# A graph-network layer on one Trainium2 core: twelve consecutive edge tiles per half of a chunk, and loads grouped to match

## Chip, cores and metric

The kernel runs on one core of a Trainium2 chip. The metric is the device time of one execution in microseconds (us); the median of several runs counts.

## The reference

There are N = 12,500 nodes with 160 features (64 scalars, 32 vectors of three) and E = 400,000 edges, sorted by destination. Cut to what matters:

```python
h_s, h_v = s @ lin1_ws * a / sqrt(64), einsum(v, lin1_wv) * a / sqrt(32)   # per node
w  = silu(edge_scalars @ fc_w1 / 8) @ fc_w2 / 8                            # per edge, 224 weights
es, ev = h_s[edge_src], h_v[edge_src]                                      # gather, random rows
mid_s, mid_v = products of w, es, ev with edge_attr (e0, e1)               # messages
agg = segment_sum(mid, edge_dst) / 4                                       # to the destinations
pre = sc(s, v) + lin2(agg) * a
out = layernorm(x + concat(silu(pre_s[:, :64]), sigmoid(pre_s[:, 64:]) * pre_v))
```

## The kernel before

Edges are cut into 3125 tiles of 128. Three consecutive tiles make a block (`BT = 3`, 1042 blocks, each 384 edges by destination), and a block's destinations are taken to lie within a window of 16 nodes from its first one. A chunk has 24 tiles in two halves of twelve (`SIDE`), since the edge scalars have 64 rows and two halves fill 128 partitions (`es`). A step (`steps`) takes a quad: two neighbouring slots of each half. `tile_of` says which tile sits in a slot: in before, half 0 holds the even blocks and half 1 the odd ones, in groups of three tiles. The last five tiles are put into steps of their own. There are 782 steps.

**Start.** Node tables are computed block by block (`h_tab`, 12,500 rows of 640 bytes, written to DRAM by ACT's queue). Meanwhile POOL gathers the source rows of 25 quads from `x` itself (`raw_rows`, L360, 100 gathers; their columns of `src` come with `load_raw_columns`, L241 to L250); these quads are turned into rows of `h` later, in the steps 30, 60, ... 750 (`raw_stages`). `rel`, the destination within the window, is computed for all tiles at once (`relative`, L510, through `by_slots`).

**Main loop** (from L1232). The order of all engines is written out by hand; each engine works through its queue in that order, and waits come from the data. Per step:
- POOL gathers one row of `h_tab` per edge, one instruction per tile of 128 rows (`gather`, L549), into `hg`, a buffer with four copies (`deep`, `bufs=4`).
- PE multiplies the hidden layer by the weights (`weights`, L561, four matmuls into `pw`); the hidden layer (`hidden`, L540/L542) is made four steps ahead, every second step, from `es`.
- DVE makes the products `pr` (L571, L579), the one-hot of `rel` (`one_hot`, L616) and from it and the edge attributes the selection `sel` (`select_quad`, L630).
- PE sums a tile's messages into its block's window (`sum_up`, `add_tile`, L637). A pair of blocks shares an accumulator `pa`: block b of half 0 in its upper rows, b + 1 of half 1 in its lower ones. When both are complete, ACT copies it out (`close`, L1116), two steps later PE turns it (`turn_blocks`, L646), and after 16 blocks `output` (L662) applies `lin2`; DVE adds each block's result to its window of `acc` (L670).
- Every four tiles of 128 nodes whose blocks are all added (`settled`) are finished in a job of its own (`begin`, `finish`).

21 quads are fetched without POOL: their rows come one by one in small transfers issued by SP and ACT (`Off`, `hs_sp`, `hs_act`, L946), spread over the steps before; `Off.begin` (L901 to L914) loads the four columns of `src` for such a quad, one load per run of consecutive tiles. With the 25 raw quads, 46 steps therefore have no gather on POOL.

SP's queue also carries the edge scalars (`load_chunk`, L217, eight steps ahead, `es` has two copies) and, for `AHEAD` = 60 tiles at a time, the indices `idx` and the edge attributes `eat` (`ahead`, L178/L179, twelve steps ahead; `idx` has two copies, `eat` one). ACT copies `eat` into the order of the slots (`by_slot`, `eas`, L604) when the first tile of a group is needed. The queue of SP is in order: a load that waits for its buffer holds up all loads behind it.

In `load_chunk` a half is four runs of three tiles, each 1.5 KB per row:

```python
            queue.dma_start(
                to[:, :n * P].rearrange("c (q e) -> c q e", e=EB),
                bass.AP(tensor=full.tensor, offset=full.offset,
                        ap=[full.ap[0], [2 * EB, k], [1, EB]]))
```

Of the kernel before, what the change touches and what calls it, by code (L numbers as in the profile page):

```python
# [11 lines left out]
I32 = mybir.dt.int32  # L12
# [4 lines left out]
OP = mybir.AluOpType  # L17
# [4 lines left out]
P = 128  # L22
# [7 lines left out]
BT = 3  # L30
EB = BT * P
W = 16
Q = 4
SB = 4 * BT
SIDE = SB
AHEAD = 5 * SB
NF = 4

MARGIN = 128
# [6 lines left out]
ROW = 4 * D  # L46
# [8 lines left out]
RAW_FIRST = 30  # L55
RAW_EVERY = 30
RAW_STEPS = [RAW_FIRST + RAW_EVERY * r for r in range(RAWS)]
RAW_TILES = (0, 1, 3, 4)
RAW_TILE0 = Q * RAW_FIRST

CYC = [(i, (i + 1) % 3, (i + 2) % 3) for i in range(3)]
# [8 lines left out]
def gnn_kernel(  # L70
# [69 lines left out]
    CT = 2 * SIDE  # L140
    chunks = [(c, (SIDE, SIDE)) for c in range(0, TT - CT + 1, CT)]
    left = len(chunks) * CT
    if left < TT:
        assert BT <= TT - left < 2 * BT
        chunks.append((left, (BT, TT - left - BT)))

    def tile_of(c, half, u):
        return chunks[c][0] + u // BT * 2 * BT + half * BT + u % BT

    steps = []  # L150
    for c, (_, halves) in enumerate(chunks):
# [33 lines left out]
    def index(t):  # L185
        a0, idx, _ = ahead(t)
        return idx[:, t - a0:t - a0 + 1]

    def by_slots(out, of, n, f):


        m = n // SB
        for u in range(2 * BT if m else 0):
            o, i = out[:, u // 2 * Q + u % 2:u // 2 * Q + u % 2 + 1], of[:, u // BT * 2 * BT + u % BT:][:, :1]
            f(bass.AP(tensor=o.tensor, offset=o.offset,
                      ap=[o.ap[0], [SB * o.ap[1][0], m], [2 * o.ap[1][0], 2], *o.ap[2:]]),
              bass.AP(tensor=i.tensor, offset=i.offset,
                      ap=[i.ap[0], [SB * i.ap[1][0], m], [BT * i.ap[1][0], 2], *i.ap[2:]]),
              u // BT * 2, m)
        return m * SB  # L200

    ess = {}

    def load_chunk(c, queue=nc.sync):
        if c in ess:
            return
        t0, halves = chunks[c]
        es = ess[c] = loads.tile([2 * S, SIDE * P], F32, name="es")
        for half, n in enumerate(halves):
            to = es[half * S:(half + 1) * S]  # L210
            e0 = (t0 + half * BT) * P
            if n < BT:
                queue.dma_start(to[:, :n * P], es_t[:, e0:e0 + n * P])
                continue
            k = n // BT
            full = es_t[:, e0:e0 + EB]
# [4 lines that stand above are left out]
# [1 line left out]

    ident = consts.tile([P, P], F32, name="ident")
    make_identity(nc, ident)
    iota_i = consts.tile([P, P], I32, name="iota_i")
    nc.gpsimd.iota(iota_i, pattern=[[1, P]], base=0, channel_multiplier=0)

    eps = consts.tile([P, 1], F32, name="eps")
# [1 line left out]

    assert all(T % 6 == 0 for T in RAW_STEPS)
    raw_of = {T: r for r, T in enumerate(RAW_STEPS)}
    raw_cols = consts.tile([P, RAWS, 5], I32, name="raw_cols")
    hi_of = consts.tile([P, RAWS * Q], F32, name="hi_of")
    lo_rows = consts.tile([RAWS * Q, P], F32, name="lo_rows")
    row_of = consts.tile([P, 1], F32, name="row_of")
# [1 line left out]
    l1v = consts.tile([V3, V3], F32, name="l1v")  # L238
    nc.vector.memset(l1v, 0.0)

    def load_raw_columns(a, b):  # L241

        for r in range(a, b):
            t = steps[RAW_STEPS[r]][2][0][0]
            assert [u for u, _, _ in steps[RAW_STEPS[r]][2]] == [t + k for k in RAW_TILES]
            assert divmod(t, GT) == (r, RAW_TILE0 - 5 * r) and t + 5 <= (r + 1) * GT
        of = src[a][:, RAW_TILE0 - 5 * a:][:, :5]
        nc.sync.dma_start(raw_cols[:, a:b],
                          bass.AP(tensor=of.tensor, offset=of.offset,
                                  ap=[of.ap[0], [P * GT - 5, b - a], [1, 5]]))  # L250

    w1 = consts.tile([2 * S, 2 * S], F32, name="w1")
    nc.vector.memset(w1, 0.0)
# [30 lines left out]
    with tc.tile_pool(name="nodes", bufs=3) as nodes, tc.tile_pool(  # L284
# [45 lines left out]
            nc.vector.tensor_reduce(early, share, AX.X, OP.min)  # L330
            nc.vector.tensor_scalar(early, early, -float(MARGIN), None, op0=OP.is_lt)

        load_raw_columns(0, 4)
        at = consts.tile([P, NT], F32, name="at")
        nc.scalar.dma_start(at, attr)
        l1 = consts.tile([P, P], F32, name="l1")
# [89 lines left out]
        def scale():  # L426

            nc.vector.tensor_copy(iota_p, iota_i)
            part = ends_pool.tile([P, RAWS * Q], I32, name="part")
            parts = part.rearrange("p (r a b) -> p r a b", a=2, b=2)  # L430
            of = bass.AP(tensor=raw_cols.tensor, offset=raw_cols.offset,
                         ap=[raw_cols.ap[0], [5, RAWS], [3, 2], [1, 2]])
            nc.vector.tensor_scalar(parts, of, P.bit_length() - 1, None,
                                    op0=OP.logical_shift_right)
            nc.vector.tensor_copy(hi_of, part)
            nc.vector.tensor_scalar(parts, of, P - 1, None, op0=OP.bitwise_and)
            nc.vector.tensor_copy(lo_of, part)
            diagonal = ends_pool.tile([P, P], F32, name="diagonal")
            nc.vector.tensor_mul(diagonal, ident, iota_p)
            nc.vector.tensor_reduce(row_of, diagonal, AX.X, OP.add)  # L440
            at_c = 0
            for a, b in ((64, 128), (0, 64), (192, 224), (160, 192), (128, 160)):
                nc.vector.tensor_scalar_mul(w2[:, at_c:at_c + b - a], raw[:, a:b],
                                            1.0 / math.sqrt(64))
                at_c += b - a
            for m, of, by in scales:
                nc.vector.tensor_scalar_mul(m, of, by)
# [60 lines left out]
    def relative(out, of, b0, m):  # L508
        l = lo[:, b0:b0 + 1]
        nc.vector.tensor_tensor(  # L510
            out, of, bass.AP(tensor=l.tensor, offset=l.offset,
                             ap=[l.ap[0], [4 * l.ap[1][0], m], [l.ap[1][0], 2]]), op=OP.subtract)

    for t in range(by_slots(rel, dt, TT, relative), TT):
        nc.vector.tensor_tensor(rel[:, slot_of[t]:slot_of[t] + 1], dt[:, t:t + 1],
                                lo[:, t // BT:t // BT + 1], op=OP.subtract)
    ends.close()
# [80 lines left out]
    def by_slot(t):  # L598

        a0, _, eat = ahead(t)  # L600
        if a0 not in sorted_eat:
            n = min(AHEAD, TT - a0)
            eas = loads.tile([P, AHEAD, 4], F32, name="eas")
            m = by_slots(eas, eat, n, lambda o, i, b0, m: nc.scalar.copy(o, i))  # L604
            for k in range(m, n):
                o = slot_of[a0 + k] - a0
                nc.scalar.copy(eas[:, o], eat[:, k])
            sorted_eat[a0] = eas
        return sorted_eat[a0]
# [231 lines left out]
    with tc.tile_pool(  # L841
# [46 lines left out]
        class Off:  # L888
# [11 lines left out]

            def begin(self, T, slots):  # L901

                cols = loads.tile([P, Q], I32, name="cols")
                tiles = [steps[T][2][k][0] for k in slots]
                nc.vector.memset(cols, 0.0) if len(tiles) < Q else None
                k = 0
                while k < len(tiles):
                    g, u = divmod(tiles[k], GT)
                    m = 1
                    while k + m < len(tiles) and tiles[k + m] == tiles[k] + m and u + m < GT:  # L910
                        m += 1
                    nc.sync.dma_start(cols[:, k:k + m], src[g][:, u:u + m])
                    k += m
                return cols  # L914

            def byte(self, cols):

                at_byte = loads.tile([P, Q], F32, name="at_byte", bufs=1)
                nc.vector.tensor_scalar(at_byte, cols, float(ROW), None, op0=OP.mult)
                return at_byte  # L920

            def turn(self, at_byte):
# [196 lines left out]
        def turn_blocks(n, j, sa, beside=nc.scalar.copy):  # L1119
            if not turns:  # L1120
                tts[0] = late.tile([P, 7, NO, W], F32, name="tt", bufs=1)
                tts[1] = late.tile([V, NO, W], F32, name="t3", bufs=1)
            turned(misc_ps, sa, tts[0], tts[1], len(turns), 2, beside)
            turns.extend((2 * j, 2 * j + 1))
            if len(turns) == NO or NB - 2 * j - 2 in (10, 4, 0):
                done = list(turns)
                turns.clear()
                maps_due.append((n + 1, done))
# [28 lines left out]
        def sum_up(n, tiles, pr, sel):  # L1157

            for slot, (t, half, _) in sorted(enumerate(tiles), key=lambda k: (k[1][2], k[1][1])):
                b = t // BT  # L1160
                j = b // 2
                assert b % 2 == half
                if j not in pas:
                    pas[j] = pa_ps.tile([P, 512], F32, name="pa")
                added[b] += 1
                stop = added[b] == min(BT, TT - b * BT)
                add_tile(pas[j], half, sel, slot, pr[:, slot], start=(added[b] == 1), stop=stop)
                if stop:
                    ended.add(b)
                    if {2 * j, 2 * j + 1} <= ended:  # L1170
                        close(j, n)

        def add_up(n):
# [276 lines left out]
```

## Time and profile before

| | |
|---|---|
| median of 3 runs | 3861.9 us (3860.59 to 3872.28) |
| the profiled execution | 3860.29 us, span 3858.5 us |
| busy: PE / DVE / ACT / POOL | 3365.6 / 2450.9 / 1023.9 / 2877.1 us |
| mean granted TensorE clock | 0.951 |
| moved | 430.39 MB, mean 112 GB/s |

The time of an execution is a little longer than its span, which runs from the first to the last instruction. Busy time is what an engine spends inside instructions; the time in which it takes up the next one, or waits, is outside. In the rows of groups the columns are: line, engine, operation, written and read tile with shapes, count, busy time in us and mean in ns, idle time just before and what ended it. In the lists of waits: who waited, what it waited for, us in total, how many times, the longest. In a timeline: start and duration in us, engine, line, operation, and in brackets the idle time before it and what ended it. A `q` behind an engine's name is its queue, which issues transfers.

### The profile page before, as it was taken

The numbers are of one execution on the slowest core, as the hardware profiler recorded it, in microseconds if no ns is written. First come the engines' busy times: TensorE is split into PE (matmuls) and PEld (weight loads), VectorE is DVE, ScalarE is ACT, GpSimd is POOL, SyncE is SP. The second block draws the span as 40 slices with busy tenths as digits, with TensorE's granted clock in tenths as the row PEclk, the third lists the DMA queues.
The fourth block names the chain that finished last, engine by engine and source line by source line (L and its number), as shares of the span: only waits on it lengthen the run. The fifth ranks groups of instructions, "written<-read, shape, count | busy, mean of one in ns | idle before, by whom it ended". The sixth has DMA issues, their size and how long they took to land. (4 is left out here: it accounts for less than half of the span.)

```text
span 3858.5 us, 79139 instructions
## 1 busy us (share of the span) xinstructions
PE 3365.6 (87%) x18417; PEld 1697.8 (44%) x18417; DVE 2450.9 (64%) x6839; ACT 1023.9 (27%) x3246; POOL 2877.1 (75%) x3046
## 2 busy tenths in 40 slices
PE   3588988998988998998898898998999998988897
PEld 3234444444444444444444444444444444444444
DVE  2465666666656666666666566666666666666666
ACT  0222222223222222232222222222222322222222
POOL 7777776777777777777777777777777777777775
PEclk7799999999999999999999999999999999999999
DMA  9744444445445454444544444445454544445442
GB/s 217 222 101 107 106 105 109 103 105 113 105 99 117 102 113 105 110 105 107 112 103 114 104 102 110 105 102 114 103 111 105 113 100 110 112 102 113 107 97 71
DMA packets 328137, 430.39 MB, mean 112 GB/s; under 512 B 96368, under 2 KB 270988, under 8 KB 326764
## 3 DMA queue, kind: packets, MB, share of 16 engines
q0 software_dynamic: 145824, 249.07, 28.7%
q1 hardware_dynamic: 153988, 154.65, 18.1%
q10 hardware_dynamic: 27848, 21.56, 1.9%
q8 instruction: 148, 2.42, 0.3%
q14 instruction: 329, 2.70, 0.2%
HBM read 400.80 MB, written 24.19 MB: 110 GB/s over the span
## 5 line engine op out<-in xcount | busy, mean ns | idle before, releaser
L549 POOL DMA_INDIRECT hg<-h_tab,idx x2938 | 2779.7, 946 | 918.8 <-issue 794.1
L637 PE MATMUL pa<-pr,sel 128*64 128x416 f32 x6250 | 1324.2, 546 | 3.9 <-DVE sel L630 3.9
L579 DVE TENSOR_TENSOR pr<-pw,hg 128x384 f32<-128x384 f32 x2205 | 1090.8, 547 | 0.0
L561 PE MATMUL pw<-w,hid 64*128 64x224 f32 x6250 | 829.9, 384 | 199.5 <-DVE sel L630 170.6
L571 DVE TENSOR_TENSOR pr<-pw,hg 128x512 f32<-128x512 f32 x735 | 507.9, 691 | 723.1 <-DMA hg<-h_tab,idx 688.6
L561 PEld LDWEIGHTS pw<-w,hid 64*128 64x128 f32 x6250 | 548.2, 191 | 471.5 <-DVE sel L630 220.6
L637 PEld LDWEIGHTS pa<-pr,sel 128*64 128x64 f32 x6250 | 392.4, 140 | 578.9 <-issue 537.9
L540 PE MATMUL ph<-es,w 128*128 128x512 f32 (+1 forms) x784 | 457.3, 666 | 36.2 <-DVE acc L1093 29.0
L1116 ACT COPY sa<-pa 128x416 f32<-128x416 f32 x521 | 262.0, 503 | 648.3 <-PE pa L637 591.4
L542 ACT ACTIVATE hid<-ph 128x512 f32<-128x512 f32 x392 | 233.3, 595 | 694.3 <-PE ph L540 389.1
L616 DVE TENSOR_TENSOR pw<-rel,pw 128x64 f32<-128x64 int16 x782 | 175.1, 224 | 347.8 <-PE pw L561 338.8
L646 PE MATMUL pt<-ident,sa 128*128 128x128 f32 (+1 forms) x2084 | 329.7, 281 | 62.0 <-ACT hid L542 36.4
L646 PEld LDWEIGHTS pt<-ident,sa 128*128 128x128 f32 (+1 forms) x2084 | 218.5, 131 | 344.3 <-issue 200.7
L650 ACT COPY tt<-pt 128x192 f32<-128x192 f32 x521 | 165.6, 318 | 643.9 <-PE pt L646 269.8
L662 PE MATMUL po<-tt,l 128*96 128x256 f32 (+3 forms) x1340 | 317.1, 384 | 10.3 <-DVE y L749 4.6
L630 DVE TENSOR_TENSOR sel<-pw,eas 128x256 f32<-128x256 f32 (+1 forms) x757 | 311.8, 412 | 0.2
L662 PEld LDWEIGHTS po<-tt,l 128*96 128x96 f32 x1340 | 211.3, 166 | 121.3 <-issue 48.3
L540 PEld LDWEIGHTS ph<-es,w 128*128 128x128 f32 (+1 forms) x784 | 121.6, 195 | 309.3 <-issue 177.3
L670 DVE TENSOR_TENSOR acc<-acc,os 96x32 f32 x1042 | 194.1, 186 | 21.1 <-ACT os L665 2.6
L360 POOL DMA_INDIRECT raw_rows<-in_x_dram,raw_cols x100 | 95.5, 955 | 35.7 <-issue 27.4
L665 ACT COPY os<-po 96x512 f32<-96x512 f32 (+2 forms) x67 | 38.1, 569 | 274.4 <-PE po L662 271.8
L700 PE MATMUL pp<-ident,acc 96*128 96x96 f32 x190 | 37.4, 282 | 83.4 <-DVE pw L616 65.5
(141 smaller groups left out, 1401.2 us busy)
## 6 DMA issues: line engine op xcount, KB each, us to landing
es<-in_es_t_dram SPq DMA_DIRECT2D x260, 384.0 KB
hs_sp<-h_tab SPq DMA_DIRECT2D x5632, 0.6 KB
hs_act<-h_tab ACTq DMA_DIRECT2D x5376, 0.6 KB
hg<-h_tab,idx POOLq DMA_INDIRECT x2938
raw_tab<-raw_rows ACTq DMA_DIRECT2D x25, 320.0 KB
rg<-raw_tab SPq DMA_DIRECT2D x25, 320.0 KB
h_tab<-ht ACTq DMA_DIRECT2D x6, 1280.0 KB
xt<-in_x_dram SPq DMA_DIRECT2D x23, 320.0 KB
```

The costliest lines, as they stand in the source:

```text
L540: nc.tensor.matmul(ph[:k, c], w1[:k, :k], es[:k, t0 * P + c0 * P:t0 * P + c1 * P], start=True, stop=True)
L542: nc.scalar.activation(hid[:k, c], ph[:k, c], AF.Silu, scale=1.0 / math.sqrt(64))
L549: nc.gpsimd.indirect_dma_start(out=hg[:, t, :], out_offset=None, in_=h_tab, in_offset=bass.IndirectOffsetOnAxis(ap=i, axis=0))
L561: nc.tensor.matmul(pw[:, t, :NWT], hid[r, c * P:(c + 1) * P], w2[r], start=True, stop=True)
L571: nc.vector.tensor_mul(two, pw[:, :n, :2 * S].rearrange("p t (k c) -> p t k c", k=2), hg[:, :n, None, :S].to_broadcast([P, n, 2, S]))
L579: nc.vector.tensor_mul(pr[:, :n, first:first + V3].rearrange("p t (i c) -> p t i c", i=3), pw[:, :n, None, 2 * S + k * V:2 * S + (k + 1) * ...
L630: nc.vector.tensor_mul(sel[:, :n], oh[:, :, None, :].to_broadcast([P, n, 4, W]), e[:, :, :, None].to_broadcast([P, n, 4, W]))
L637: nc.tensor.matmul(pa[half * ROWS:(half + 1) * ROWS, :NPR], sel[:, t].rearrange("p k w -> p (k w)"), pr, start=start, stop=stop)
L646: nc.tensor.transpose(pt[:c, four * P:four * P + k], sa[:k, four * P:four * P + c], ident[:k, :k])
L662: nc.tensor.matmul(po[:, k, :nb], l2[:b, terms[to, part, four]], a[:, :nb], start=(n == 0), stop=(n == len(of) - 1))
L670: nc.vector.tensor_add(window, window, os[:, :, b])
L1116: nc.scalar.copy(sa, pas.pop(j)[:, :NPR])
```

## The change

- **Order of tiles.** In 129 of the 130 chunks each half holds twelve consecutive tiles: blocks 0 to 3 of the chunk's eight in half 0, 4 to 7 in half 1 (`WIDE`, `tile_of`). Blocks b and b + 4 share an accumulator (`place_of`, `pair_blocks`); before it was b and b + 1. The last full chunk and the five tiles behind it keep the old order.
- **Edge scalars.** A half of such a chunk is one run of 6 KB per row.
- **Groups.** `AHEAD` is 72 tiles, three chunks; ACT copies a group's attributes with four strided copies (`by_wide_slots`) where it took six.
- **Columns of a quad.** The four tiles of a quad are now t, t+1, t+12, t+13 (`RAW_TILES`). `Off.begin` loads the 14 columns from t to t+13 in one transfer where they lie in one row group of `src`; `load_raw_columns` does the same for the raw quads, the first two of them in two loads.
- **Relative destinations.** Six strided operations for the wide chunks, and six for the 24 tiles of the last full chunk.
- **Memory.** `iota_i` and `raw_cols` (now 14 columns per quad) move from the constants to the scratch that is freed after the start; `cols` has 14 columns.

```diff
-AHEAD = 5 * SB
+AHEAD = 6 * SB
-RAW_TILES = (0, 1, 3, 4)
+RAW_TILES = (0, 1, SIDE, SIDE + 1)
...
+    WIDE = left // AHEAD * AHEAD // CT
     def tile_of(c, half, u):
+        if c < WIDE:
+            return chunks[c][0] + half * SIDE + u
         return chunks[c][0] + u // BT * 2 * BT + half * BT + u % BT
+    PER = SIDE // BT
+    def place_of(b):
+        if b < 2 * PER * WIDE:
+            return b // (2 * PER) * PER + b % PER, b // PER % 2
+        return b // 2, b % 2
...
+    def by_wide_slots(out, of, n, f):
+        m = n // CT
+        for half in range(2):
+            for k in range(2):
+                f(strided(out, 2 * half + k, [(CT, m), (Q, SIDE // 2)]),
+                  strided(of, half * SIDE + k, [(CT, m), (2, SIDE // 2)]))
...
     def load_chunk(c, queue=nc.sync):
...
+            if c < WIDE:
+                e0 = (t0 + half * SIDE) * P
+                queue.dma_start(to, es_t[:, e0:e0 + SIDE * P])
+                continue
...
-    iota_i = consts.tile([P, P], I32, name="iota_i")
+    iota_i = ends_pool.tile([P, P], I32, name="iota_i")
-    raw_cols = consts.tile([P, RAWS, 5], I32, name="raw_cols")
+    NC = SIDE + 2
+    raw_cols = ends_pool.tile([P, RAWS, NC], I32, name="raw_cols")
...
-        load_raw_columns(0, 4)
+        load_raw_columns(0, 2, 0, 2)
+        load_raw_columns(0, 2, SIDE, 2)
+        load_raw_columns(2, 4)
...
-    for t in range(by_slots(rel, dt, TT, relative), TT):
+    T0 = WIDE * CT
+    for a in range(2):
+        for u in range(BT):
+            u += a * BT
+            nc.vector.tensor_tensor(
+                strided(rel, u // 2 * Q + u % 2, [(CT, WIDE), (2, 2), (BT * Q, SIDE // (2 * BT))]),
+                strided(dt, u, [(CT, WIDE), (SIDE, 2), (2 * BT, SIDE // (2 * BT))]),
+                strided(lo, a, [(2 * PER, WIDE), (PER, 2), (2, SIDE // (2 * BT))]), op=OP.subtract)
+    for t in range(T0 + by_slots(rel[:, T0:], dt[:, T0:], TT - T0,
+                                 lambda o, i, b0, m: relative(o, i, T0 // BT + b0, m)), TT):
...
-            m = by_slots(eas, eat, n, lambda o, i, b0, m: nc.scalar.copy(o, i))
+            if a0 + n <= WIDE * CT:
+                by_wide_slots(eas, eat, n, nc.scalar.copy)
+                m = n
...
             def begin(self, T, slots):
-                cols = loads.tile([P, Q], I32, name="cols")
                 tiles = [steps[T][2][k][0] for k in slots]
+                g, u = divmod(tiles[0], GT)
+                if tiles == [tiles[0] + k for k in RAW_TILES] and u + NC <= GT:
+                    cols = loads.tile([P, NC], I32, name="cols")
+                    nc.sync.dma_start(cols, src[g][:, u:u + NC])
+                    return strided(cols, 0, [(SIDE, 2), (1, 2)])
...
-            turns.extend((2 * j, 2 * j + 1))
+            turns.extend(pair_blocks[j])
...
-                j = b // 2
-                assert b % 2 == half
+                j, of_half = place_of(b)
+                assert of_half == half
-                    if {2 * j, 2 * j + 1} <= ended:
+                    if set(pair_blocks[j]) <= ended:
                         close(j, n)
```

More of the change, by code (lines that the diff above doesn't have):

```diff
@@ L147, in tile_of @@
     def tile_of(c, half, u):
+        if c < WIDE:
+            return chunks[c][0] + half * SIDE + u
         return chunks[c][0] + u // BT * 2 * BT + half * BT + u % BT
+    PER = SIDE // BT
[3 more added lines that the diff above has]
+        return b // 2, b % 2
+    pair_blocks = {}
+    for b in range(NB):
+        j, half = place_of(b)
+        assert half == len(pair_blocks.setdefault(j, []))
+        pair_blocks[j].append(b)
     steps = []
@@ L187, in index, with strided @@
         return idx[:, t - a0:t - a0 + 1]
+    def strided(a, k, dims):
+        a = a[:, k:k + 1]
+        return bass.AP(tensor=a.tensor, offset=a.offset,
+                       ap=[a.ap[0], *[[a.ap[1][0] * d, n] for d, n in dims], *a.ap[2:]])
     def by_slots(out, of, n, f):
@@ L193, in by_slots @@
         for u in range(2 * BT if m else 0):
[L194 to L198, printed above, removed]
+            f(strided(out, u // 2 * Q + u % 2, [(SB, m), (2, 2)]),
+              strided(of, u // BT * 2 * BT + u % BT, [(SB, m), (BT, 2)]),
               u // BT * 2, m)
         return m * SB
+    def by_wide_slots(out, of, n, f):
+        m = n // CT
+        assert m * CT == n
+        for half in range(2):
+            for k in range(2):
+                f(strided(out, 2 * half + k, [(CT, m), (Q, SIDE // 2)]),
+                  strided(of, half * SIDE + k, [(CT, m), (2, SIDE // 2)]))
     ess = {}
@@ L239, in gnn_kernel, with load_raw_columns @@
     nc.vector.memset(l1v, 0.0)
-    def load_raw_columns(a, b):
+    def load_raw_columns(a, b, k=0, n=NC):
         for r in range(a, b):
@@ L245, in load_raw_columns @@
             assert [u for u, _, _ in steps[RAW_STEPS[r]][2]] == [t + k for k in RAW_TILES]
-            assert divmod(t, GT) == (r, RAW_TILE0 - 5 * r) and t + 5 <= (r + 1) * GT
-        of = src[a][:, RAW_TILE0 - 5 * a:][:, :5]
-        nc.sync.dma_start(raw_cols[:, a:b],
+        g, u = divmod(RAW_TILE0 + a * Q * RAW_EVERY + k, GT)
+        assert u - (GT - Q * RAW_EVERY) * (b - a - 1) >= 0 and u + n <= GT
+        of = src[g][:, u:u + n]
+        nc.sync.dma_start(raw_cols[:, a:b, k:k + n],
                           bass.AP(tensor=of.tensor, offset=of.offset,
-                                  ap=[of.ap[0], [P * GT - 5, b - a], [1, 5]]))
+                                  ap=[of.ap[0], [P * GT - (GT - Q * RAW_EVERY), b - a], [1, n]]))
     w1 = consts.tile([2 * S, 2 * S], F32, name="w1")
@@ L431, in scale @@
             of = bass.AP(tensor=raw_cols.tensor, offset=raw_cols.offset,
-                         ap=[raw_cols.ap[0], [5, RAWS], [3, 2], [1, 2]])
+                         ap=[raw_cols.ap[0], [NC, RAWS], [SIDE, 2], [1, 2]])
             nc.vector.tensor_scalar(parts, of, P.bit_length() - 1, None,
@@ L603, in by_slot @@
             eas = loads.tile([P, AHEAD, 4], F32, name="eas")
-            m = by_slots(eas, eat, n, lambda o, i, b0, m: nc.scalar.copy(o, i))
+            if a0 + n <= WIDE * CT:
+                by_wide_slots(eas, eat, n, nc.scalar.copy)
+                m = n
+            else:
+                assert a0 >= WIDE * CT
+                m = by_slots(eas, eat, n, lambda o, i, b0, m: nc.scalar.copy(o, i))
             for k in range(m, n):
@@ L901, in begin @@
             def begin(self, T, slots):
-                cols = loads.tile([P, Q], I32, name="cols")
                 tiles = [steps[T][2][k][0] for k in slots]
+                g, u = divmod(tiles[0], GT)
[3 more added lines that the diff above has]
+                    return strided(cols, 0, [(SIDE, 2), (1, 2)])
+                cols = loads.tile([P, NC], I32, name="cols")[:, :Q]
                 nc.vector.memset(cols, 0.0) if len(tiles) < Q else None
@@ L913, in begin @@
                     k += m
-                return cols
+                return cols.rearrange("p (a b) -> p a b", b=2)
             def byte(self, cols):
                 at_byte = loads.tile([P, Q], F32, name="at_byte", bufs=1)
-                nc.vector.tensor_scalar(at_byte, cols, float(ROW), None, op0=OP.mult)
+                nc.vector.tensor_scalar(at_byte.rearrange("p (a b) -> p a b", b=2), cols,
+                                        float(ROW), None, op0=OP.mult)
                 return at_byte
```

## The prediction

> **What bounds the kernel now.** I read the page first, then the waits and the timeline of POOL, and last the timelines of the start and of the places where POOL stood.
>
> ```profile
> span 3858.5 us, 79139 instructions
> PE 3365.6 (87%) x18417; PEld 1697.8 (44%) x18417; DVE 2450.9 (64%) x6839; ACT 1023.9 (27%) x3246; POOL 2877.1 (75%) x3046
> ...
> L549 POOL DMA_INDIRECT hg<-h_tab,idx x2938 | 2779.7, 946 | 918.8 <-issue 794.1
> L360 POOL DMA_INDIRECT raw_rows<-in_x_dram,raw_cols x100 | 95.5, 955 | 35.7 <-issue 27.4
> ```
>
> PE has the largest busy share, but POOL's 75% misleads: its idle time is nearly all "issue", and 2779.7 busy plus 918.8 idle on L549 make 3698.5 of the 3858.5 us. The timeline and the waits of POOL show what this idle time is (start, duration, engine, and in brackets the idle time before it):
>
> ```profile
> 3.32 1.10 POOL L360 DMA_INDIRECT raw_rows<-in_x_dram,raw_cols  x1 [0.87 <-DMA raw_cols<-in_src_dram]
> ...
> 133.98 0.95 POOL L549 DMA_INDIRECT hg<-h_tab,idx  x1 [0.30 <-issue]
> 135.23 1.89 POOL L549 DMA_INDIRECT hg<-h_tab,idx  x1 [0.30 <-issue]
> ...
> 399.61 0.95 POOL L549 DMA_INDIRECT hg<-h_tab,idx  x1 [0.30 <-issue]
> 400.86 0.95 POOL L549 DMA_INDIRECT hg<-h_tab,idx  x1 [0.30 <-issue]
> ...
> 3831.19 0.94 POOL L549 DMA_INDIRECT hg<-h_tab,idx  x1 [0.30 <-issue]
> ```
>
> ```profile
> POOL hg L549 <- issue: 794.1, 2603, 0.6
> POOL hg L549 <- DMA hg<-h_tab,idx: 43.0, 141, 0.3
> POOL hg L549 <- DVE pr L579: 38.3, 52, 5.1
> ...
> POOL raw_rows L360 <- DMA raw_rows<-in_x_dram,raw_cols: 7.4, 9, 1.6
> ```
>
> POOL issues one gather of 128 rows every 1.25 us (399.61 to 400.86): 0.95 of work and a gap of 794.1/2603 = 0.305. The chain is: first gather at 3.3; 100 x (0.955 + 0.305) = 126.0; 2938 x (0.946 + 0.305) = 3675.4; waits beyond the normal gap, for a free gather buffer 38.3 - 52 x 0.305 = 22.4 and for earlier raw gathers 7.4 - 9 x 0.305 = 4.7. These make 3831.8, and the last gather ends at 3832.1. Behind it lie 26.4 us of last sums and stores. So 98.5% of the span is a count of gathers times a fixed period. Even the step from raw rows to h_tab at 133.98 shows no wait. The other engines matter only where they fall four gather buffers behind: 22.4 us in all.
>
> This execution took 3860.3 us (span 3858.5, 1.8 around it); the median of the runs shown is 3861.9, 1.6 higher. I predict for the median.
>
> **The change part by part.** It removes no gather: the steps, their four tiles and the quads that are fetched otherwise stay as many, so the 3801 us of gathers stay. PE, too, has the same matmuls in the same shapes: two slots per half and step, a pair of blocks closing after the same slots, sixteen blocks per output. Followed through the code's queues, all outputs come at the same steps; of the 24 finishing jobs 15 start one step later, since a pair now holds b and b+4, and the last starts at the same step (773). What is left are loads, small copies and set-up.
>
> ```profile
> q0 software_dynamic: 145824, 249.07, 28.7%
> q1 hardware_dynamic: 153988, 154.65, 18.1%
> ```
>
> ```profile
> L912 SPq DMA_DIRECT2D cols<-in_src_dram x50: 356/422/632, 129.0 to 3633.6; - x50
> ```
>
> *Edge loads.* In 129 chunks each half becomes 64 runs of 6 KB, where it was 256 of 1.5 KB: 258 x 192 = 49,536 runs fewer, the same bytes and issues. The transfer engines are 28.7 + 18.1% busy, so faster loads free no path. The rates per engine, 249.07 MB / (0.287 x 3858.5 x 16) = 14.1 GB/s for the gathers and 13.8 for q1, with its longer and its shorter runs, also leave little to gain. Value 0; the bounds are in the rivals. *SP issues:* by the code 50 column loads become 25, and 75 pairs of idx and eat loads become 68; at the 0.42 us of the row, (25 + 14) x 0.42 = 16 us of SP issue over the whole run, against no POOL wait on idx or cols in its list. Value 0. The shared eat buffer is now reloaded 6 steps after its copies, not 3, so less is queued behind that wait on SP.
>
> ```profile
> L604 ACT COPY eas<-eat 128x40 f32<-128x40 f32 x312 | 44.5, 220 | 19.0 <-issue 17.7 <-DMA es<-in_es_t_dram 1.2
> ```
>
> *Edge attributes.* 312 copies of 40 elements become 43 x 4 = 172 of 72, and 6 short ones for the last group. If one takes as long as before it is 172 x 0.220 = 38 us, if it grows with its elements 172 x 0.396 = 68, against 44.5 now; either is at most 24 us spread over the run, on an engine busy for 27%. Four in a row hold up what ACT has queued behind them, a hid or sa copy, by 1.6 us at most, where six now take 1.3. Value 0.
>
> ```profile
> 0.74 0.46 SPq L248 DMA_DIRECT2D raw_cols<-in_src_dram  x1
> ...
> 128.57 0.41 SPq L688 DMA_DIRECT2D xt<-in_x_dram  x1
> ```
>
> ```profile
> SPq L688 <- DMA h_tab<-ht: 10.7, 1, 10.7
> ```
>
> *Start on SP.* Two more column loads stand ahead of the node loads: 2 x 0.46 = 0.9 us, and if the second has to wait until the first has landed (0.74 to 3.32) 2.6 more, 3.5 at worst. The table stores have landed by 128.57, when the load that waited for them goes out; the first gather from the table is at 133.98. So 5.4 us cover 3.5; without that cover each us would be paid in full. The first raw gather needs only the first load and stays. The third, two periods on at 5.8, needs the second load: issued at 1.2 it has landed at 3.8, issued at 3.3 at 5.9. Cost 0 to 0.1, I take 0.
>
> ```profile
> L510 DVE TENSOR_TENSOR rel<-dt,lo 128x520 int16<-128x520 int32 x6 | 7.1, 1360 | 13.5 <-DMA dt<-in_dst_dram 13.5
> ...
> L515 DVE TENSOR_TENSOR rel<-dt,lo 128x1 int16<-128x1 int32 x5 | 0.4, 172 | 0.0
> ```
>
> ```profile
> 147.84 0.23 DVE L616 TENSOR_TENSOR pw<-rel,pw 128x64 f32<-128x64 int16 x1 [7.69 <-PE pw L561]
> ```
>
> *Relative destinations.* Six operations of 520 elements become six of 516, and six small ones are added at 172 ns: 1.0 us on DVE. Behind it DVE idles 7.69 for PE, so it costs the path nothing. But the gather at 135.23 beside these operations took 1.89, not 0.95; one more such overlap costs 0.95, one fewer gains it. I take 0. The scratch that moves into the part freed after the start is last read by POOL before 133.98, ahead of the steps that overwrite it.
>
> *Stalls.* So the sum of the change is 0 (-1 to +1 in the start), and what can move are the 22.4 us in which POOL found all gather buffers full. The largest are worth a look:
>
> ```profile
> 1474.33 0.69 DVE L571 TENSOR_TENSOR pr<-pw,hg 128x512 f32<-128x512 f32 x1 [2.96 <-DMA hg<-h_tab,idx]
> ...
> 1476.61 4.55 PE L662 MATMUL po<-tt,l 128*96 128x256 f32 x10 [3.53 <-DVE y L749]
> ...
> 1492.37 0.95 POOL L549 DMA_INDIRECT hg<-h_tab,idx  x1 [3.92 <-DVE pr L579]
> ...
> 2274.99 2.40 PE L662 MATMUL po<-tt,l 128*96 128x256 f32 x10 [1.17 <-ACT hid L542]
> ```
>
> DVE waits 2.96 us for rows, PE idles 3.53 us, its next ten matmuls take 4.55 and not 2.40, and POOL, which may run on until all buffers are full, stands 3.92 ahead of the gather at 1492.37: late rows turn into slow matmuls, and these into a stall. (The Trainium skill, TensorE: Matmul & The Clock Gate, in the table of why this matters for your kernels, says that idle gaps of TensorE over about 3 us throw it back to half clock; these two rows, 3.53 and 1.17 us of idling ahead of 4.55 and 2.40, agree.) Steps and outputs are where they were, so I expect most of these stalls again: 22 us, moved by some us where a finishing job starts a step later. Ends for the range: 13 us of them gone, or 15 more.
>
> **The rivals.** *A, faster: the stalls go.* Fewer runs and fewer copies leave rows and copies earlier, PE never idles over 3 us, and POOL never finds its buffers full: 3861 - 22.4 = 3839. For it speaks the chain at 1474 to 1492; against it that the steps with a gap in POOL's work and the outputs stay where they are. Half of the stalls gone would be 3850. Chance of over 0.3% (11.6 us): 0.09.
>
> *B, slower: the bursts of longer runs hold up the gathers.* Rows of a gather get their turn on a transfer engine behind runs of 6 KB. At 13.8 GB/s such a run takes 0.44 us and one of 1.5 KB 0.11. It decides from the point where POOL itself must wait for earlier gathers to drain, as it did in the start: 9 waits, 4.7 us beyond the gap, 0.52 each. One such wait per chunk would be 130 x 0.52 = 68 us: 3929. Against it: in the main loop the 141 waits on earlier gathers are 43.0/141 = 0.305 each, the normal gap, so there is room. Chance 0.05. (The Trainium skill, DMA: Bandwidth & Descriptors, section on queues, rings and completion order, states that each transfer engine takes turns between its queues at packet granularity; by that rule longer packets on SP's queue do lengthen the gathers' turns. No run here shows yet what a packet is for these runs.)
>
> *C, slower: later rows, more slow matmuls.* As B, but the rows only land later, and DVE and PE pay: each idle time of PE over some 3 us ahead of an output costs a stall of about 4 us, as at 1492. From three more of them on the loss is over 0.3%; ten would make 3901. Chance 0.05.
>
> *D: the long runs are cut up again on their way.* Then the loads do what they did, and the time is the forecast's, 3861; its chance, 0.1, is part of the forecast's.
>
> **How the numbers follow.** 0.3% of 3862, 11.6 us, is about what a measurement of this kernel can tell from no change. Forecast with D: 3861 us (3860.3 + 0, and half of the 1.6 to the median), chance 0.81. A has 0.09; B and C have 0.05 each. For the range I take the forecast with the ends of the stalls: 3861 - 13 = 3848 and 3861 + 15 = 3876, which leaves out about 2 in 10.
>
> **What would show it.** Right: L549 again 2938 gathers of 946 ns at a period of 1.25, the waits on DVE pr near 38 us in total, the first table gather near 134, the last ending near 3832; about 50,000 packets fewer on q1 (D: as many as before); 178 copies in the eas group. Wrong: POOL waits on hg transfers longer than 0.31 (B); more outputs at 4 us and a longer total on DVE pr (C); hardly any wait on DVE pr (A); a first table gather after 136.

## The result, and the profile after

| | before | after |
|---|---|---|
| median, 20 runs each | 3865.05 us (3859.76 to 3872.28) | 3869.79 us (3866.26 to 3875.16) |
| ratio | | 1.0013 [1.0007, 1.0019] |
| the profiled execution | 3860.29 us, span 3858.5 | 3871.78 us, span 3870.0 |

The change costs 4.7 us, 0.13%. The time lies inside the forecast's range, and the loss is below the 0.3% that I took for the limit of what can be told; but the interval is ±0.06% and does not hold 1. A small loss is there where my sum said 0. (Of the 8.8 us between the forecast of 3861 and the result, 4.1 lie in the kernel before: its median is 3865.05 over 20 runs and was 3861.9 over three.) The rest of this document is about the 4 to 5 us of the change. Some of the runs below fell on chips where the kernel before itself takes 5559 us and POOL waits for DVE through most of the run; from those only the durations in their profiles are used.

The page of after, parts 1, 3 and 5, and then the list of POOL's waits:

```profile
span 3870.0 us, 78900 instructions
PE 3382.1 (87%) x18417; PEld 1702.2 (44%) x18417; DVE 2456.8 (63%) x6845; ACT 1012.6 (26%) x3112; POOL 2888.3 (75%) x3046
...
q1 hardware_dynamic: 99124, 154.85, 16.7%
...
L595 POOL DMA_INDIRECT hg<-h_tab,idx x2938 | 2790.8, 950 | 919.1 <-issue 790.7
```

```profile
POOL hg L595 <- issue: 790.7, 2590, 0.6
POOL hg L595 <- DMA hg<-h_tab,idx: 48.0, 157, 0.3
POOL hg L595 <- DVE pr L625: 36.9, 51, 8.2
```

L595 is the gather (L549 before). As many instructions as before, and the idle time before them is the same (919.1 against 918.8). Its busy time grew by 2790.8 - 2779.7 = 11.1 us, and the span by 11.5. So POOL waits no longer than before: the gathers themselves take longer, somewhere. The timelines of POOL and of DVE around the first gathers from the table show one place:

```profile
133.39 0.95 POOL L595 DMA_INDIRECT hg<-h_tab,idx  x1 [0.30 <-issue]
134.65 1.57 POOL L595 DMA_INDIRECT hg<-h_tab,idx  x1 [0.30 <-issue]
136.52 2.02 POOL L595 DMA_INDIRECT hg<-h_tab,idx  x1 [0.31 <-issue]
138.85 2.00 POOL L595 DMA_INDIRECT hg<-h_tab,idx  x1 [0.30 <-issue]
141.16 2.03 POOL L595 DMA_INDIRECT hg<-h_tab,idx  x1 [0.30 <-issue]
143.49 2.02 POOL L595 DMA_INDIRECT hg<-h_tab,idx  x1 [0.30 <-issue]
145.81 2.02 POOL L595 DMA_INDIRECT hg<-h_tab,idx  x1 [0.30 <-issue]
148.13 0.95 POOL L595 DMA_INDIRECT hg<-h_tab,idx  x1 [0.30 <-issue]
```

```profile
133.41 14.08 DVE L555 TENSOR_TENSOR rel<-dt,lo 128x516 int16<-128x516 int32 x6 [14.52 <-DMA dt<-in_dst_dram]
...
147.84 0.23 DVE L667 TENSOR_TENSOR pw<-rel,pw 128x64 f32<-128x64 int16 x1
```

```profile
L555 DVE TENSOR_TENSOR rel<-dt,lo 128x516 int16<-128x516 int32 x6 | 14.1, 2658 | 14.5 <-DMA dt<-in_dst_dram 14.5
```

Before had a second lengthened gather, two behind the one at 135.23:

```profile
138.67 1.90 POOL L549 DMA_INDIRECT hg<-h_tab,idx  x1 [0.30 <-issue]
```

The six wide operations for `rel` take 14.08 us where the six of before took 7.1, with 516 elements against 520. Six gathers beside them are lengthened, the first to 1.57 us and the other five to 2.0, and their ends (138.54, 140.85, 143.19, ...) are 2.3 us apart, as the operations are: 14.08/6 = 2.3. (The mean of 2658 ns is more than that because each operation's time overlaps the end of the one before it.) Together the six take 11.66 us where 6 x 0.946 = 5.68 is normal: 6.0 us too long. Before, two gathers were lengthened, to 1.89 and 1.90, by 1.9 in all. That is +4.1 us on POOL, and POOL sets the end. The idle time of 7.69 that DVE had ahead of its first one-hot (L667) is gone as well: the one-hot starts at 147.84 in both kernels.

The other 11.1 - 4.1 = 7.0 us are 2.4 ns on each gather, everywhere. The first experiments show that this comes and goes between executions of one kernel.

### The profile page after: what moved, and what is told of

Its sections match the earlier page's. It is cut to its first block, busy times and chain, and to the rows that moved or that the text cites. A ratio compares the mean times of both kernels' runs of the same rounds, so it can differ in the third digit from the quotient of the medians.

```text
span 3870.0 us, 78900 instructions
## 1 busy us (share of the span) xinstructions
PE 3382.1 (87%) x18417; PEld 1702.2 (44%) x18417; DVE 2456.8 (63%) x6845; ACT 1012.6 (26%) x3112; POOL 2888.3 (75%) x3046
## 3 DMA queue, kind: packets, MB, share of 16 engines
q1 hardware_dynamic: 99124, 154.85, 16.7%
## 5 line engine op out<-in xcount | busy, mean ns | idle before, releaser
L595 POOL DMA_INDIRECT hg<-h_tab,idx x2938 | 2790.8, 950 | 919.1 <-issue 790.7
L667 DVE TENSOR_TENSOR pw<-rel,pw 128x64 f32<-128x64 int16 x782 | 174.8, 224 | 342.1 <-PE pw L607 331.8
```

Source lines behind the costliest of these rows:

```text
L595: nc.gpsimd.indirect_dma_start(out=hg[:, t, :], out_offset=None, in_=h_tab, in_offset=bass.IndirectOffsetOnAxis(ap=i, axis=0))
```

## The experiments

Line numbers shift from kernel to kernel; the gather and the operations for `rel` are known by their tiles.

**Both kernels once more, unchanged.** `before_again`:

> The kernel before, unchanged: what two profiles of one kernel differ by. If the mean period of the undisturbed gathers, 1.2504 us in the first profile, is a property of the kernel, it is 1.2504 again (+-0.0005); if it is a property of the execution, it lies anywhere from 1.250 to 1.253, worth up to 8 us over 3010 gathers. The six operations on rel lengthen two gathers by 0.95 us each.

`after_again`:

> The changed kernel, unchanged. Theory lock (the six operations on rel, now with three free dimensions, take turns with POOL's gathers, and each lengthens one by about 1 us): again six long gathers, 6 us together against 1.9 before, and 4 to 5 us over the kernel before in time. Theory period (the longer runs or the other traffic lengthen every gather by 2.7 ns, 8 us): the period is 1.253 again while that of before stays at 1.250. Both can hold in part.

Measured on the same chip, against before at 3860.09 us: before again 3860.99, 1.0004 [0.9995, 1.0013]; after again 3865.48, 1.0015 [1.0007, 1.0024]. The gather's row of the page, of before again and then of after again, and below them POOL's timeline of after again beside the operations for `rel` (the first and the last of six long gathers):

```profile
L549 POOL DMA_INDIRECT hg<-h_tab,idx x2938 | 2786.4, 948 | 913.6 <-issue 792.4
```

```profile
L595 POOL DMA_INDIRECT hg<-h_tab,idx x2938 | 2784.3, 948 | 918.4 <-issue 799.5
```

```profile
135.83 2.25 POOL L595 DMA_INDIRECT hg<-h_tab,idx  x1 [0.30 <-issue]
...
147.68 2.01 POOL L595 DMA_INDIRECT hg<-h_tab,idx  x1 [0.30 <-issue]
```

An unchanged before can have 2786.4, 6.7 more than in its first profile. It has two lengthened gathers again, but one of them is the last gather from `x` (1.69, at 133.26) and is not in this row; the other is of 1.89. An after can have all other gathers as short as the first profile of before: 2784.3 less the 6.6 of its six long ones is 2777.7, and 2779.7 less 1.9 is 2777.8. So the 7.0 us spread over all gathers come and go with the execution. The six long gathers stay, and so does the loss.

**Undo one part: `rel` with two free dimensions.** In after, the six operations of 129 x 2 x 2 elements become twelve of 129 x 2:

```diff
-    for a in range(2):
-        for u in range(BT):
-            u += a * BT
-            nc.vector.tensor_tensor(
-                strided(rel, u // 2 * Q + u % 2, [(CT, WIDE), (2, 2), (BT * Q, SIDE // (2 * BT))]),
-                strided(dt, u, [(CT, WIDE), (SIDE, 2), (2 * BT, SIDE // (2 * BT))]),
-                strided(lo, a, [(2 * PER, WIDE), (PER, 2), (2, SIDE // (2 * BT))]), op=OP.subtract)
+    for u in range(SIDE):
+        nc.vector.tensor_tensor(
+            strided(rel, u // 2 * Q + u % 2, [(CT, WIDE), (2, 2)]),
+            strided(dt, u, [(CT, WIDE), (SIDE, 2)]),
+            strided(lo, u // BT, [(2 * PER, WIDE), (PER, 2)]), op=OP.subtract)
```

> The changed kernel with the six operations of 516 elements in three free dimensions on rel replaced by twelve of 258 in two, the same elements. Theory lock, if the third dimension is what makes them take turns: at most two to four gathers lengthened, 2 us together, and the time 4 us below that of the changed kernel, at that of before. If any operation with these operands takes its turn, twelve shorter ones lengthen up to twelve gathers by some 0.5 us, and nothing is gained. Theory period: no change beyond 1 us.

Measured: 3858.63 us, 0.9996 [0.9987, 1.0005]; its interval and that of after again, on the same chip, do not meet. The group of these operations (columns as in part 5 of the page), the gather's row of the page, and POOL's timeline beside the operations:

```profile
L553 DVE TENSOR_TENSOR rel<-dt,lo 128x258 int16<-128x258 int32 x12 | 7.2, 792 | 15.2 <-DMA dt<-in_dst_dram 15.2
```

```profile
L593 POOL DMA_INDIRECT hg<-h_tab,idx x2938 | 2779.1, 946 | 919.6 <-issue 796.6
```

```profile
136.92 1.27 POOL L593 DMA_INDIRECT hg<-h_tab,idx  x1 [0.30 <-issue]
138.50 1.39 POOL L593 DMA_INDIRECT hg<-h_tab,idx  x1 [0.30 <-issue]
140.20 0.95 POOL L593 DMA_INDIRECT hg<-h_tab,idx  x1 [0.30 <-issue]
141.45 1.39 POOL L593 DMA_INDIRECT hg<-h_tab,idx  x1 [0.30 <-issue]
```

Twice the instructions, half the time: 7.2 us for the same elements. Three gathers are lengthened, by 4.05 - 3 x 0.946 = 1.2 us in all, and the gathers' total falls by 2784.3 - 2779.1 = 5.2. All else of the change is in this kernel, and it runs like before.

**Do that part alone: before, with three free dimensions.** The same elements of before's six operations, taken as 130 x 2 x 2 in place of 260 x 2:

```diff
-    for t in range(by_slots(rel, dt, TT, relative), TT):
...
+    CTS = TT // CT
+    for u in range(2 * BT):
+        nc.vector.tensor_tensor(
+            three(rel, u // 2 * Q + u % 2, [(CT, CTS), (2, 2), (SB, 2)]),
+            three(dt, u // BT * 2 * BT + u % BT, [(CT, CTS), (BT, 2), (SB, 2)]),
+            three(lo, u // BT * 2, [(8, CTS), (1, 2), (4, 2)]), op=OP.subtract)
+    for t in range(CTS * CT, TT):
```

> The kernel before with its six operations on rel written in three free dimensions (130 x 2 x 2 in place of 260 x 2, the same elements in the old order), nothing else. Theory lock by the third dimension: six gathers of about 2.0 us, the operations 14 us together in place of 7, and 4 us more time than before. Theory period: as before within 1 us.

Measured: 3864.12 us, 1.0010 [1.0001, 1.0018]. The group, and from POOL's timeline the first and the last of six lengthened gathers:

```profile
L521 DVE TENSOR_TENSOR rel<-dt,lo 128x520 int16<-128x520 int32 x6 | 14.2, 2679 | 14.0 <-DMA dt<-in_dst_dram 14.0
```

```profile
136.89 2.07 POOL L560 DMA_INDIRECT hg<-h_tab,idx  x1 [0.30 <-issue]
...
148.61 2.04 POOL L560 DMA_INDIRECT hg<-h_tab,idx  x1 [0.30 <-issue]
```

The order of tiles, the loads and the copies are those of before, and the loss is there: 7.1 us of operations become 14.2, and six gathers are long, by 6.6 us in all. In time the loss is only just clear of none, since the interval starts at 1.0001; the rows are plain.

**Is it the order of the dimensions?** In after, the long dimension (129) is put innermost, 2 x 2 x 129 where it was 129 x 2 x 2; run twice.

```diff
-                strided(rel, u // 2 * Q + u % 2, [(CT, WIDE), (2, 2), (BT * Q, SIDE // (2 * BT))]),
+                strided(rel, u // 2 * Q + u % 2, [(2, 2), (BT * Q, SIDE // (2 * BT)), (CT, WIDE)]),
...
```

> The changed kernel with the same six operations on rel, their three dimensions in another order: 2 x 2 x 129 in place of 129 x 2 x 2. If short inner rows are what costs, the operations take 1.2 us or less, at most two or three gathers are longer, 2 us together, and the time is 4 to 6 us below that of the changed kernel. If any third dimension makes the operations take turns with the gathers: six long gathers and the changed kernel's time.

> The changed kernel with the three dimensions in the order 2 x 2 x 129, a second time, for the time on a chip where the kernel before takes 3860 us: six long gathers again, and the changed kernel's time, 5 us over the kernel before. If the order of the dimensions mattered, it would be near the kernel before.

Both fell on chips of the 5559 us kind (5579.54 and 5564.47), so their times say nothing here. Of the first, one row of POOL's waits, the group, and from POOL's timeline the first and the last of six long gathers:

```profile
POOL hg L595 <- DVE pr L625: 1757.6, 349, 13.8
```

```profile
L555 DVE TENSOR_TENSOR rel<-dt,lo 128x516 int16<-128x516 int32 x6 | 14.3, 2720 | 11.5 <-DMA dt<-in_dst_dram 11.5
```

```profile
207.78 2.03 POOL L595 DMA_INDIRECT hg<-h_tab,idx  x1 [0.30 <-issue]
...
219.56 2.05 POOL L595 DMA_INDIRECT hg<-h_tab,idx  x1 [0.30 <-issue]
```

This other order changes nothing: 14.3 us, and six gathers of 2.03 to 2.06. It leaves a rival open. In the forms of two dimensions the innermost step in `rel` is 2 elements; in all forms of three that were run it is 12 or 24. So the runs do not tell the number of dimensions from the steps, and "three free dimensions" below stands for these forms as they are. Three dimensions are not slow as such: the products `pr`, 4 x 2 x 64 float32 elements with 64 of them side by side and one input in PSUM, take 691/512 = 1.35 ns an element:

```profile
L617 DVE TENSOR_TENSOR pr<-pw,hg 128x512 f32<-128x512 f32 x735 | 507.9, 691 | 726.3 <-DMA hg<-h_tab,idx 707.1
```

**The operation by itself.** Does the gather slow the operation, or is it slow alone? `tail_ops` is `rel_two_dims` with nine more operations behind the last gather, 96 x 516 elements each from and to SBUF, in three forms in turn.

```diff
...
+            for _ in range(3):
+                for forms in ((((SB, 258), (2, 2)), ((SB, 258), (BT, 2)), ((4, 258), (1, 2))),
+                              (((CT, 129), (2, 2), (SB, 2)), ((CT, 129), (SIDE, 2), (2 * BT, 2)),
+                               ((8, 129), (4, 2), (2, 2))),
+                              (((2, 2), (SB, 2), (CT, 129)), ((SIDE, 2), (2 * BT, 2), (CT, 129)),
+                               ((4, 2), (2, 2), (8, 129)))):
+                    o, i, l = forms
+                    nc.vector.tensor_tensor(strided(rel[:V3], 0, o), strided(whole, 0, i),
+                                            strided(flat, 4096, l), op=OP.subtract)
```

> The variant with rel in two dimensions, and behind the last store's issue, where POOL gathers no more, nine operations of 516 elements of rel's kind (int32 minus float32 to int16, all in SBUF, 96 partitions, results not used): three times the form of two dimensions (258 x 2), of three (129 x 2 x 2), and of three with the long one innermost (2 x 2 x 129). Theory slow form (three free dimensions are slow by themselves, and a gather beside one lasts until its end): about 1.15, 2.3 and under 1.2 us each, with no gather near. Theory turns (the operation is as fast as before, but waits for the gather as the gather waits for it): about 1.15 us each, all three. Only the profile counts here.

The timeline of DVE, first round: two dimensions, three, and three with the long one inside:

```profile
5549.95 1.29 DVE L1409 TENSOR_TENSOR rel<-acc 96x516 int16<-96x516 int32 x1
...
5551.27 2.46 DVE L1409 TENSOR_TENSOR rel<-acc 96x516 int16<-96x516 int32 x1
...
5553.77 2.52 DVE L1409 TENSOR_TENSOR rel<-acc 96x516 int16<-96x516 int32 x1
```

With no gather near, the two forms with three free dimensions take 2.46 and 2.52 us where the one with two takes 1.29: 4.8 and 4.9 ns an element against 2.5. The operation is slow by itself, and the gather beside it is the one that suffers.

**Keep the slow operations, take away what they share with the gather.** If length alone did the harm, a gather beside any operation of 2.3 us would be long. In `rel_psum` the operations of after keep their three dimensions, but the subtracted row `lo` is copied once to PSUM and read there (for 128 of the 129 chunks), so only one input comes from SBUF.

```diff
...
+    lo_ps = lo_pool.tile([P, 1024], F32, name="lo_in_psum")
+    nc.vector.tensor_copy(lo_ps, lo[:, :1024])
+    for c0, n, base in ((0, 128, lo_ps), (128, WIDE - 128, lo)):
...
-                strided(lo, a, [(2 * PER, WIDE), (PER, 2), (2, SIDE // (2 * BT))]), op=OP.subtract)
+                    strided(base, c0 * 2 * PER + a, [(2 * PER, n), (PER, 2), (2, SIDE // (2 * BT))]),
+                    op=OP.subtract)
```

> The changed kernel with its operations on rel in the slow form, but with the subtracted row (1024 of 1042 blocks) read from PSUM, where one copy puts it before; six small operations for the last chunk read it from SBUF. If the gathers are held up by an operation's second input from SBUF, no gather is longer than 0.95 us beside the six, whatever these take, and the time is 5 to 6 us below that of the changed kernel. If any operation of DVE of this length holds them up, six long gathers remain and the time is the changed kernel's.

> The changed kernel with the slow three-dimensional operations on rel, the subtracted row read from PSUM, a second time. On a chip where the kernel before takes 3860 us: no long gather beside the operations, though these still take 2.3 us each and 14 us together. The first products come some us later, which the gather buffers cover. Time 6 us below the changed kernel, 1 to 2 below the kernel before (3858). If what the changed kernel lost were DVE's own 7 us more and not the gathers, the time would stay at the changed kernel's, 3865.

> The changed kernel with the slow operations on rel reading their subtracted row from PSUM, once more, for its time where the gathers set the pace (the kernel before at 3860 us): no long gather beside the operations, 5 to 7 us below the changed kernel. If DVE's own longer work were the loss: the changed kernel's time. Where the kernel before takes some 5560 us, POOL waits for DVE through the whole run, and the time tells nothing of the start.

The first two fell on 5559 us chips (5563.26 and 5564.26); in the profile of the first, every gather beside the operations takes 0.95. The third ran against before at 3860.03: 3858.07 us, 1.0001 [0.9992, 1.0010]. Its group, and POOL's timeline beside and behind it:

```profile
L560 DVE TENSOR_TENSOR rel<-dt,lo_in_psum 128x512 int16<-128x512 int32 x6 | 13.9, 2631 | 13.4 <-DMA dt<-in_dst_dram 13.4
```

```profile
135.84 0.95 POOL L601 DMA_INDIRECT hg<-h_tab,idx  x1 [0.30 <-issue]
...
154.79 0.94 POOL L601 DMA_INDIRECT hg<-h_tab,idx  x1 [1.74 <-DVE pr L631]
```

The operations are as slow as in after (13.9 us), and no gather is lengthened. So it is not DVE's time as such: a gather, which reads its indices `idx` from SBUF, is held up by an operation that reads two tiles from SBUF. (The Trainium skill, SBUF — State Buffer, section Who interferes with whom, says that a DVE instruction with two SBUF inputs contends with a GpSimd instruction that reads SBUF, and that one with at most one such input, outside the modes in which DVE uses both ports, does not. These rows agree: 2.02 us with both in SBUF, 0.95 with one in PSUM.) After itself shows the same of a longer operation with one input: DVE's reduction of `rel` (L913) runs for 3.40 us from 247.48 on, and the gathers at 248.37 and 249.62, which lie wholly beside it, take 0.95 and 0.94.

What is left of the slow operations in `rel_psum` is the last row of its timeline: DVE starts its products later, and POOL finds its buffers full once, for 1.74 - 0.30 = 1.44 us. That is at most the price of the length, against 6.0 with the contention. Part of the delay belongs to this version: between the last operation for `rel` and the one-hot at 151.87 DVE makes two copies into `pw` and idles 2.00 us for PE, and after has neither there. The run was on another chip than after again, and the two intervals overlap a little, so in time alone this run is weaker than `rel_two_dims`; the rows of the gathers are plain.

**Both remedies.** Twelve operations of two dimensions, with `lo` in PSUM.

> The changed kernel with rel in twelve two-dimensional operations and the subtracted row in PSUM: both remedies. If only the long gathers cost, it is as fast as the one with PSUM alone, and 1 us faster than the one with two dimensions alone, whose three long gathers lose 1.2 us: 3857 to 3858 where the kernel before takes 3860. If the operations' length counts too, it is below both.

> Both remedies, once more: twelve two-dimensional operations and the subtracted row in PSUM. No long gather beside the operations, which take 7 us together. Where the kernel before takes 3860 us: 3857 to 3858, at most 1 us from the one with PSUM alone.

The first fell on a 5559 us chip (5570.11). The second took 3857.65 against 3860.03, 0.9993 [0.9984, 1.0002]. The group, and one of the gathers beside it in POOL's timeline:

```profile
L558 DVE TENSOR_TENSOR rel<-dt,lo_in_psum 128x256 int16<-128x256 int32 x12 | 7.2, 787 | 13.4 <-DMA dt<-in_dst_dram 13.4
```

```profile
134.36 0.95 POOL L599 DMA_INDIRECT hg<-h_tab,idx  x1 [0.30 <-issue]
```

No gather beside them is long and POOL has no new wait there. Its median is the lowest of the versions, but its interval holds 1: it cannot be told from before, nor from the other two remedies. By the rows at most the 1.9 us that before loses here could be won.

## Why the prediction was wrong, and where it was right

**What bounds the kernel: right.** In every profile on the chips of the 3860 us kind the 2938 gathers at 0.945 to 0.950 us and their gap of 0.305 (790.7/2590) fill nearly all of the span, and the loss showed up as longer gathers on POOL.

**Relative destinations: the step that failed.** "Six operations of 520 become six of 516" priced them by their elements, at the 1360 ns of the row. The row was for two free dimensions and the diff shows three, with other steps; they measured 2658 ns. Then "behind it DVE idles 7.69 for PE, so it costs the path nothing" asked for DVE's successor only. The row that mattered stood beside it in my text, the gather of 1.89 at 135.23: I saw that these operations lengthen gathers (one, as I read it; there were two), bounded it by one overlap more or fewer (±0.95), and did not let the number of overlaps follow the length of the operations. Two long gathers became six, +4.1 us in the first pair of profiles and 6.6 - 1.7 = 4.9 in the second; the medians say 4.7 and 5.4. That the time still lies in the range is luck: the range was wide for the stalls, which did not move, and the terms of the change itself had ±1.

**Edge loads, SP issues, edge attributes: right, worth nothing that can be measured.** The packets on q1 fell by 153988 - 99124 = 54,864 (about 50,000 expected), which refutes rival D. The copies became 178 as counted, and their mean of 248 ns fell between my two ends (220 and 396). The group, durations as least, median and most:

```profile
L228 ACT COPY eas<-eat x172: 240/247/263, 140.9 to 3727.1; 128x72 f32<-128x72 f32 x172
```

With the operations for `rel` mended all this together stands at 0.9996 [0.9987, 1.0005].

**Start on SP: right in its sum, one wait not foreseen.** The first gather from the table came at 133.39 (133.98 before, "near 134"). But `xt`'s load stood for earlier raw gathers, whose freed scratch had moved (the waits of SP's queue, and its timeline):

```profile
SPq L739 <- DMA raw_rows<-in_x_dram,raw_cols: 16.1, 1, 16.1
```

```profile
145.43 0.41 SPq L739 DMA_DIRECT2D xt<-in_x_dram  x1
```

It held SP's queue until 145.43 (128.57 before). POOL shows no wait in that stretch, so it cost nothing that can be seen. It was not tried alone, but `rel_two_dims` has the same wait (`xt` at 148.96) and runs like before.

**Stalls: right.** POOL's waits for `pr` are 36.9 us in 51 against 38.3 in 52 ("near 38"), so rivals A and C did not come. Waits on gathers in flight are 48.0/157 = 0.306 each, the normal gap: rival B did not come either. The last gather ends at 3842.97 and not near 3832: of the 10.8 us between, some 4 are the long gathers and 7 the execution's.

**The bound of 0.3%** was too coarse for this many runs: 20 of each kernel told 0.13% from nothing.

## What to carry to other kernels

Price a vector operation by its access pattern as well as by its elements: when the pattern gains a dimension or its steps change, look for a row of that form, and where there is none take twice as long as an end of the range. An engine with idle time is not free to be slow while it shares something with the engine that sets the end: count how many of the bounding engine's instructions start beside the longer one, and price each by a lengthened row if the profile has one. Both remedies are cheap: split the operation so that each part keeps the faster form, or let one input come from PSUM.

## What the runs showed of the hardware that I had not expected

- A subtraction of int32 and f32 to int16 over strided elements takes 4.8 to 4.9 ns an element in the two forms with three free dimensions and 2.5 in the one with two (2.46, 2.52 and 1.29 us for 516). Whether the dimension or the steps do it stays open.
- A gather beside the slow form with both inputs in SBUF lasts 2.00 to 2.07 us in place of 0.95 (the first of a row 1.57 to 2.25), beside one with an input in PSUM 0.95. Beside shorter ones with both in SBUF (1.14 us apart before, 0.6 in `rel_two_dims`) only some gathers are held, for 1.69 to 1.90 and 1.27 to 1.39.
- Which ones are held can be read from the starts in the profiles of before, before again and `rel_two_dims`: those that go free start between 0.05 us ahead of an operation and 0.02 behind it (137.42 and 137.42 in before, 140.20 and 140.25 in `rel_two_dims`), the held ones 0.02 behind it or later. A held gather ends 0.7 to 0.9 us behind the start of the next operation, in these and in after. That looks as if it waited for the running operation to end; no run moved the starts to test it.
- The gathers' own duration differs by 2.4 ns between executions of one kernel, 7 us in sum: the difference of one pair of profiles (11.5 us) was more than twice that of the medians (4.7).
